# Where the routing's transpose stands in the tiles of a gated FFN

## The chip, the cores and the metric

The kernel runs on one core of one Trainium2 chip. The metric is the device time of one execution, in microseconds (us). The kernel before takes 975.53 us, the median of 3 runs (974.83 to 975.91).

## The reference, cut to what matters

The block works on one sequence of 2048 tokens with 1024 channels: half an FFN, an attention with a convolution in front, and half an FFN again. Both FFNs use the same weights and are alike. The cut below leaves the attention out.

```python
def ffn(xf):                       # xf: 2048 x 1024, after a layer norm
    routing = softmax(xf @ gate_w.T)                 # 2048 x 8
    in_scale = routing @ in_channel_scale            # 2048 x 1024
    out_scale = routing @ out_channel_scale          # 2048 x 1024
    return (xf * in_scale) @ sign(weight).T * out_scale + bias
x = x + 0.5 * ffn(layernorm(x))
x = x + attention(layernorm(x))
x = x + 0.5 * ffn(layernorm(x))
```

So each token gets a routing of 8 numbers; from it come a scale for each input channel and one for each output channel; between the two stands a product with a 1024 x 1024 matrix of signs.

## The kernel before, in words

The core's engines are TensorE (PE, with its weight loads listed as PEld), VectorE (DVE), ScalarE (ACT), GpSimd (POOL) and the DMA queues, SyncE's (SP) among them. Each engine works through its own list in order, and waits for the others by semaphores.

Each FFN is an object of the class `Ffn`. It runs over 16 tiles of 128 tokens. What is done for a tile, with the lines of the kernel before:

- `norm`: the layer norm of a row of tokens (statistics on DVE, L164 to L170; the row itself on ACT, L182).
- `transpose`: eight PE transposes of 128 x 128 (tile `tr_f`, L216), copied out by ACT (L217).
- `gate`: the gate's products, sixteen on PE in four groups of 32 columns of the array (tile `lgp_f`, L224), copied out by ACT (L232).
- `route`: one small product (L237), then the softmax on DVE and ACT (L239 to L249). The result is `rhl_f`, the routing with its rounding rest, repeated eight times.
- `turn`: one PE transpose of the routing (tile `rt_f`, L256) and one DVE copy that brings it to SBUF and rounds it (tile `rT_f`, L258). This is "the routing's turn".
- `scale`: eight small products that read `rT_f` and use 32 rows of the array each (tile `is_f`, L268), and in `out_scale` two more for the output's scale (`po_f`, L291). DVE multiplies the transposed row by the input scale (L279), ACT rounds it to the high part of `y_f` (L281), POOL makes the low part (L282). ACT writes the output scale `os_f` (L293).
- `main`: the sign products. For each half of the output channels there are 16 products of 128 x 128 by 512 columns (8 chunks, high and low part) that add up in one PSUM bank (`pm_f`, L307). Then the sums are used: DVE multiplies the bank by the output scale (L319) and adds it to the row (L320).

`run` is the loop over tiles. In step t it calls: the gate of tile t + 2, the scale of tile t + 1, `main` of tile t for half 0, the route of t + 2, the transposes of t + 3, the norm of t + 4, and then `main` of tile t for half 1. Into this second half the turn of tile t + 2 is put by the argument `beside`: a step that `main` calls ahead of a given chunk, here chunk 6 of 8, so after 12 of the 16 products. At t = 14 and 15 there is no turn left. The first FFN's first tiles are written by hand in `begin`, and its `run` starts at t = 2; the second FFN's starts at t = 0, so they make 12 and 14 of these turns.

In `begin` the order is the written one. Everywhere else the framework's scheduler sets the order of each engine's list: it goes by the written order, by its own estimate of when an operand is there, and by the buffers, and it may take later work ahead of an instruction that it expects to wait. Instructions given to `pin` keep their place. The first FFN's DVE list also has the attention's own preparations (its layer norm, L164 to L170 on `x`, and the convolution's transforms, L460 to L462); the second FFN's has none of these.

PSUM is handed out in four pools of two banks: `mm` for the sign products, `acc` for `po_f`, `tr` for the transposes and `is_f`, `sm` for `lgp_f`, the route's product and `rt_f`.

Of the kernel before, what the change touches and what calls it, by code (L numbers as in the profile page):

```python
# [24 lines left out]
def kernel(  # L25
# [28 lines left out]
    DC = D // P  # L54
# [18 lines left out]
    def bank(kind, shape, name):  # L73
        return banks[kind].tile(shape, F32, name=name, tag=kind)
# [25 lines left out]
    def pin(ins):  # L100

        tc.keep_in_program_order(ins)
# [81 lines left out]
    class Ffn:  # L184
# [108 lines left out]
                nc.scalar.mul(osc[:, ts(h, NB)], po, 0.5)  # L293
            self.oscs[t] = osc

        def main(self, t, *halves, beside={}, apart=DC):


            y, xrow = self.ys[t], self.row(t)
            pms = {h: bank("mm", [P, NB], f"pm_{self.name}_{t}_{h}") for h in halves}  # L300
            for c, h in [(c, h) for c in range(apart) for h in halves] + [
                (c, h) for h in halves for c in range(apart, DC)
            ]:
                if h == halves[0] and c in beside:
                    beside[c]()
                for n in range(2):
                    ins = nc.tensor.matmul(  # L307
                        pms[h],
                        lhsT=y[:, n, c, :],
                        rhs=self.sw[:, c, ts(h, NB)],  # L310
                        start=(c == 0 and n == 0),
                        stop=(c == DC - 1 and n == 1),
                    )
                    if self.behind:
                        pin(ins)
                        self.behind = False
                if c == DC - 1:
                    o, xt = self.oscs[t][:, ts(h, NB)], xrow[:, ts(h, NB)]
                    nc.vector.tensor_tensor(pms[h], pms[h], o, ALU.mult)  # L319
                    nc.vector.tensor_tensor(xt, xt, pms[h], ALU.add)  # L320
                    self.leave(t, h)
            if NH2 - 1 in pms:
                del self.ys[t], self.oscs[t]
# [19 lines left out]
        def run(self, first):  # L343

            self.behind = first > self.first
            for t in range(first, self.end):
                if t + 2 not in self.lgps:
                    self.on(self.gate, t + 2)  # L350
                if t + 1 < self.end:
                    self.scale(t + 1, out=True)
                self.main(t, 0)
                self.on(self.route, t + 2)
                self.on(self.transpose, t + 3)
                self.on(self.between, t - 2)
                self.on(self.norm, t + 4, t < self.kept)
                self.on(self.add_bias, t + 4)
                self.main(t, 1, beside={DC - 2: lambda: self.on(self.turn, t + 2)})
                self.on(self.after, t - 1)  # L360
                self.beside(t)

# [719 lines left out]
```

## Time and profile before

| what | value |
|---|---|
| median of 3 runs | 975.53 us |
| the profiled execution, its own time | 974.22 us |
| its span (first to last instruction) | 972.0 us |
| PE busy | 952.3 us, 98% of the span |
| DVE busy | 638.0 us, 66% |
| ACT busy | 409.6 us, 42% |
| POOL busy | 250.4 us, 26% |
| granted TensorE clock | 1.00 over the span |
| first FFN, tiles 2 to 15 | about 47 to 195 us |
| second FFN, `run` | about 813 us to the end |

A line of the timeline gives start and length in us, the engine, the line of the kernel, the operation, output <- inputs, shapes, and the count of instructions merged; in brackets the engine's idle time before it and what ended that. The chain of work that ended last is followed back from the end: a piece gives start and length in us, then engine, tile and line. PE's instructions are pipelined, so their recorded lengths overlap: what one costs is read from start to start.

### The profile page before, as it was taken

The numbers are of one execution on the slowest core, as the hardware profiler recorded it, in microseconds if no ns is written. First come the engines' busy times: TensorE is split into PE (matmuls) and PEld (weight loads), VectorE is DVE, ScalarE is ACT, GpSimd is POOL, SyncE is SP. The second block draws the span as 40 slices with busy tenths as digits, with TensorE's granted clock in tenths as the row PEclk, the third lists the DMA queues.
The fourth block names the chain that finished last, engine by engine and source line by source line (L and its number), as shares of the span: only waits on it lengthen the run. The fifth ranks groups of instructions, "written<-read, shape, count | busy, mean of one in ns | idle before, by whom it ended". The sixth has DMA issues, their size and how long they took to land.

```text
span 972.0 us, 13861 instructions
## 1 busy us (share of the span) xinstructions
PE 952.3 (98%) x5064; PEld 623.5 (64%) x5064; DVE 638.0 (66%) x1228; ACT 409.6 (42%) x1122; POOL 250.4 (26%) x319
## 2 busy tenths in 40 slices
PE   6999999999999999999999999999999999999997
PEld 4688778876666666645555455545554556878776
DVE  5788887799986566537656455646555655666654
ACT  5586665421111111126545344536451653444441
POOL 2555443410011101004213121212122312444341
PEclk9999999999999999999999999999999999999999
DMA  9776554698487665235020430044004216646331
GB/s 337 173 199 192 154 174 145 240 246 329 153 260 204 176 172 139 77 134 203 27 104 1 169 109 5 1 157 146 1 0 154 56 31 219 171 135 174 104 109 65
DMA packets 37522, 137.21 MB, mean 141 GB/s; under 512 B 4872, under 2 KB 5896, under 8 KB 35536
## 3 DMA queue, kind: packets, MB, share of 16 engines
q1 hardware_dynamic: 28336, 98.69, 27.9%
q0 software_dynamic: 8384, 29.63, 16.1%
q10 hardware_dynamic: 736, 8.02, 2.2%
q8 instruction: 40, 0.66, 0.3%
q14 instruction: 26, 0.21, 0.1%
HBM read 81.70 MB, written 37.85 MB: 123 GB/s over the span
## 4 chain that ended last, share of the span: by engine, by line
PE 60%; issue 27%; POOL 5%; DVE 3%; DMA 2%; ACT 2%; POOLq 0%; DVEq 0%; ACTq 0%
PE pm_f L307 22%; PE cv L540 22%; POOL xr L857 3%; PE tr_f L216 3%; PE pp L991 2%; PE lgp_f L224 2%; DMA x<-in_x_dram 2%; POOL p L913 2%; PE acc L972 2%; PE is_f L268 1%; PE tr L427 1%; PE pq L880 1%; PE ao L955 1%; PE pt L942 1%; DVE st_f L164 1%
## 5 line engine op out<-in xcount | busy, mean ns | idle before, releaser
L307 PE MATMUL pm_f<-sw,y_f 128*128 128x512 f32 x1024 | 261.5, 406 | 0.6 <-ACT y_f L281 0.4
L307 PEld LDWEIGHTS pm_f<-sw,y_f 128*128 128x128 f32 x1024 | 187.1, 190 | 43.9 <-ACT y_f L281 0.8
L540 PE MATMUL cv<-v,u 128*128 128x342 f32 x576 | 166.0, 450 | 0.0
L540 PEld LDWEIGHTS cv<-v,u 128*128 128x128 f32 x576 | 109.0, 189 | 56.9 <-issue 0.3
L913 POOL TENSOR_SCALAR_AFFINE_SELECT p<-p 128x512 f32<-128x512 f32 x64 | 39.8, 646 | 280.9 <-ACT p L911 280.9
L926 ACT ACTIVATE p<-p,anm 128x128 f32<-128x128 f32 x256 | 99.0, 388 | 16.7 <-DVE anm L923 16.7
L282 POOL TENSOR_TENSOR y_f<-xnT_f,y_f 128x512 fp32r<-128x512 f32 x63 | 79.8, 1282 | 64.8 <-ACT y_f L281 64.8
L319 DVE TENSOR_TENSOR pm_f<-pm_f,os_f 128x512 f32<-128x512 f32 x64 | 44.6, 697 | 70.9 <-PE pm_f L307 70.7
L557 ACT ACTIVATE m<-cv 128x342 f32<-128x342 f32 x42 | 19.2, 457 | 158.7 <-PE cv L540 148.5
L911 ACT COPY p<-sc 128x512 f32<-128x512 f32 x64 | 34.3, 588 | 111.5 <-PE sc L901 111.4
L923 DVE TENSOR_REDUCE anm<-p 128x4 f32<-128x512 f32 x64 | 40.9, 681 | 47.6 <-POOL p L913 47.6
L972 PE MATMUL acc<-oT,wo_sb 128*128 128x512 f32 x128 | 67.2, 616 | 0.4 <-DVE oT L964 0.4
L880 PE MATMUL pq<-qkv,wq_sb 128*128 128x512 f32 x128 | 61.0, 596 | 0.0
L880 PE MATMUL pq<-qkv,wk_sb 128*128 128x512 f32 x128 | 60.1, 592 | 0.0
L540 PE MATMUL cv<-v,g 128*128 128x342 f32 (+2 forms) x224 | 57.1, 415 | 0.9 <-DVE v L462 0.9
L991 PE MATMUL pp<-pw_sb,o2T 128*128 128x512 f32 x128 | 57.4, 599 | 0.4
L864 PE MATMUL pv<-wv_sb,qkv 128*128 128x512 f32 x128 | 56.1, 592 | 0.0
L217 ACT COPY xnT_f<-tr_f 128x512 f32<-128x512 f32 x62 | 35.9, 587 | 47.7 <-PE tr_f L216 47.7
L540 PEld LDWEIGHTS cv<-v,g 128*128 128x128 f32 x224 | 39.7, 190 | 17.6 <-DVE v L462 1.3
L528 DVE SCALAR_TENSOR_TENSOR u<-g,u 128x1024 f32<-128x1024 f32 x18 | 22.0, 1220 | 41.5 <-issue 23.5
L926 ACT ACTIVATION_READ_ACCUMULATOR p<-p,anm 128x1 f32 x256 | 47.8, 187 | 0.0
L934 DVE TENSOR_TENSOR p<-p,asum 128x512 f32<-128x512 f32 x64 | 45.6, 712 | 2.2
(138 smaller groups left out, 1462.7 us busy)
## 6 DMA issues: line engine op xcount, KB each, us to landing
g<-in_conv_w_dram SPq DMA_DIRECT2D x28, 512.0 KB, 4.9
u<-in_conv_w_dram POOLq DMA_DIRECT2D x24, 512.0 KB, 6.1
x<-in_x_dram SPq DMA_DIRECT2D x16, 512.0 KB, 4.6
raw<-in_weight_t_dram SPq DMA_DIRECT2D x16, 512.0 KB, 6.0
x<-hbias POOLq DMA_DIRECT2D x16, 512.0 KB, 5.5
x<-x SPq DMA_DIRECT2D x16, 512.0 KB, 4.3
xr<-x SPq DMA_DIRECT2D x16, 512.0 KB, 6.9
x<-xr SPq DMA_DIRECT2D x16, 512.0 KB, 3.2
```

The lines of the kernel that those rows point to most:

```text
L282: lows[h].tensor_tensor(yl, y, yh.bitcast(F32), ALU.subtract)
L307: ins = nc.tensor.matmul(pms[h], lhsT=y[:, n, c, :], rhs=self.sw[:, c, ts(h, NB)], start=(c == 0 and n == 0), stop=(c == DC - 1 and n == 1),)
L319: nc.vector.tensor_tensor(pms[h], pms[h], o, ALU.mult)
L540: nc.tensor.matmul(accs[w, k][:, lo:hi], lhsT=uk[:, c, :], rhs=V[k][:, c, lo:hi], start=(c == 0), stop=(c == DC - 1),)
L864: nc.tensor.matmul(pv, lhsT=qkvs[g][2][:, c, ts(b, P)], rhs=wv_sb[:, c, ts(half, NB)], start=(c == 0), stop=(c == WC - 1),)
L880: nc.tensor.matmul(pq, lhsT=w_sb[:, c, ts(hp, P)], rhs=qkvs[g][n][:, c, :], start=(c == 0), stop=(c == WC - 1),)
L913: nc.gpsimd.affine_select(out=p, in_=p, pattern=[[0, BPG], [-1, P]], compare_op=ALU.is_ge, fill=NEG_INF, base=0, channel_multiplier=1,)
L923: nc.vector.tensor_reduce(nmax, p, AX.X, ALU.max, negate=True)
L926: nc.scalar.activation(p[:, b, :], p[:, b, :], AF.Exp, bias=nmax[:, b : b + 1], accum_out=asum[:, b : b + 1],)
L934: nc.vector.tensor_tensor(p, p, asum.unsqueeze(2).broadcast_to([P, BPG, P]), ALU.mult)
L972: nc.tensor.matmul(accs[g][m], lhsT=wo_sb[:, hp, ts(m, P)], rhs=oT, start=(hp == 0), stop=(hp == NHP - 1),)
L991: nc.tensor.matmul(pp, lhsT=o2T[:, m, ts(b, P)], rhs=pw_sb[:, m, ts(h, NB)], start=(m == 0), stop=(m == WC - 1),)
```

## The change

`main` gets an argument `behind`, a step that is called after the last product of the last half and ahead of the multiplication and the addition that use its sums. `run` gives the turn of tile t + 2 to `behind`, and no longer to `beside` ahead of chunk 6. `begin` is as it was.

```diff
-        def main(self, t, *halves, beside={}, apart=DC):
+        def main(self, t, *halves, beside={}, apart=DC, behind=lambda: None):
...
                 if c == DC - 1:
+                    if h == halves[-1]:
+                        behind()
                     o, xt = self.oscs[t][:, ts(h, NB)], xrow[:, ts(h, NB)]
                     nc.vector.tensor_tensor(pms[h], pms[h], o, ALU.mult)
...
-                self.main(t, 1, beside={DC - 2: lambda: self.on(self.turn, t + 2)})
+                self.main(t, 1, behind=lambda: self.on(self.turn, t + 2))
```

How the built lists differ, for the step that turns tile 6 of the second FFN (both are built programs; "x" counts products):

```
PE before                       PE after
pm_f_4_1 x12                    pm_f_4_1 x16
rt_f_6                          rt_f_6
pm_f_4_1 x4                     lgp_f_7 (gate)
lgp_f_7 (gate)                  pm_f_5_0 x2
is_f_6, po_f_6                  is_f_6, po_f_6
pm_f_5_0 x16                    pm_f_5_0 x14

DVE before                      DVE after
rT_f_6 (L258)                   pm_f_4_1 * os (L319)
pm_f_4_1 * os (L319)            rT_f_6 (L258)
x + pm_f_4_1 (L320)             x + pm_f_4_1 (L320)
xnT_f_6 * is_f_6 (L279) x2      xnT_f_6 * is_f_6 (L279) x2
```

So besides the moved transpose, the scheduler takes two sign products of the next tile ahead of the scale's products, and puts the copy `rT_f` behind the multiplication. This is so in 13 steps of the second FFN (tiles 2 to 14) and in 11 of the first (tiles 4 to 14; three products at tile 4). At tile 15 no gate is left. In the first FFN its scale products stood behind three products of the next tile before, and do after; in the second they stood right behind the tile's last product before, and stand behind five products of the next tile after.

In the first FFN, DVE's list has three patterns. At tiles 6 and 9 the copy stays ahead of the multiplication, but behind a statistic (L164) and a transform (L462) that stood after it before. At tile 15 the copy stays where it was, ahead of the multiplication. At the others it goes behind the multiplication; there the input's scaling (L279) also goes behind the small statistics (L168, L170). On ACT the attention's layer norm of two late tiles comes ahead of the output scale; on POOL some small operations trade places. SP's list is the same.

## The prediction

> **What bounds the kernel now.** I read the page's shares first, then who waited for whom on PE, over the whole span.
>
> ```profile
> PE 952.3 (98%) x5064; PEld 623.5 (64%) x5064; DVE 638.0 (66%) x1228; ACT 409.6 (42%) x1122; POOL 250.4 (26%) x319
> ```
>
> ```profile
> PE rt_f L256 <- DVE rhl_f L249: 2.6, 3, 1.7
> ...
> PE is_f L268 <- DVE rT_f L258: 0.3, 1, 0.3
> ```
>
> PE is busy for 98% and waits for almost nothing. So what PE issues, and in which order, is the time: a stall of PE, or a slower order, is paid in full, and nothing else is. Of the waits that the change touches, `rt_f` has 2.6 us; 1.7 of that lies in the hand-written beginning, which stays, and 0.9 in two tiles of the first FFN (0.61 at 100.5 us, 0.30 at 133.5). Between 813 us and the end PE waits for nothing at all.
>
> Next, the timeline of the second FFN where the turn and the gate stand. PE and DVE lines only:
>
> ```profile
> 881.00 0.27 PE L256 MATMUL rt_f<-ident,rhl_f 128*128 128x128 f32 x1
> ...
> 881.03 1.17 PE L307 MATMUL pm_f<-sw,y_f 128*128 128x512 f32 x4
> ...
> 881.31 0.29 DVE L258 CAST rT_f<-rt_f 128x128 fp32r<-128x128 f32 x1
> ...
> 882.13 0.38 PEld L224 LDWEIGHTS lgp_f<-xnT_f,gate_sb 128*32 128x32 f32 x16 [0.36 <-issue]
> 882.13 0.64 PE L224 MATMUL lgp_f<-xnT_f,gate_sb 128*32 128x128 f32 x16
> 882.24 0.70 DVE L319 TENSOR_TENSOR pm_f<-pm_f,os_f 128x512 f32<-128x512 f32 x1 [0.63 <-PE pm_f L307]
> ...
> 882.71 0.33 PE L268 MATMUL is_f<-rT_f,tables 32*128 32x128 f32 x2
> ...
> 882.97 0.69 DVE L320 TENSOR_TENSOR xf<-xf,pm_f 128x512 f32<-128x512 f32 x1
> ...
> 883.29 4.00 PE L307 MATMUL pm_f<-sw,y_f 128*128 128x512 f32 x16
> ```
>
> To see: the copy `rT_f` is over at 881.60, 1.1 us before the scale's products read it. And where the kind of PE work changes (full array for `pm_f`, 32 columns for the gate, 32 rows for the scale), the weight load does not run ahead: the gate's first load stands idle 0.36 us and starts with its product.
>
> Last, the chain where an order like the coming one is already there. First the beginning (gate, then sign products), then the first FFN's tile 15 (sign products, scale, sign products):
>
> ```profile
> 30.04 0.57 PE lgp_f L224 x16
> 30.61 1.16 PE pm_f L307 x4
> ```
>
> ```profile
> 175.97 1.62 PE pm_f L307 x7
> 177.59 0.26 PE is_f L268 x2
> ...
> 178.19 3.22 PE pm_f L307 x13
> ```
>
> Four undisturbed products take 0.92 us (0.231 from start to start); after the gate they take 1.16. Thirteen would take 3.00; after the scale they take 3.22. A return to the full array costs some 0.2 us, whichever kind it returns from.
>
> **The change, part by part.** Starts are from single records, us.
>
> *The transpose itself.* Before, it splits the products: product to transpose 0.240, transpose to product 0.028, then 0.314 to the next; 0.582 for two steps of 0.231, so 0.12. After, it stands between the last product and the gate. Product to transpose is again 0.24. Transpose to gate is in no undisturbed row; the nearest is transpose to a row-tiled product at 795.4 us, 0.203. The 0.44 take the place of the 0.320 from product to gate: 0.12 again. I take 0 for the move. Bounds: 0.11 (the plain step of a transpose) to 0.351 (transpose to gate at 9.0 us, where the gate also waits for a copy), so -0.09 to +0.15 a tile.
>
> *The two products that come ahead of the scale.* From the 12th product to the next tile's fourth, before: 0.582 + 2 x 0.231 + 0.320 + gate 0.371 + gate to scale 0.203 + scale 0.389 + scale to product 0.201 + first to second product 0.341 + 2 x 0.231 = 3.33. After: 4 x 0.231 + 0.237 + 0.203 + 0.371 + gate to product 0.202 (30.34 us) + 0.341 + product to scale 0.327 (177.19 and 950.89 us) + 0.389 + 0.201 + 0.341 = 3.54. So +0.205 a tile, all from one more return to the full array. 24 tiles have it (11 and 13): **+4.9 us**. At tile 15 of the second FFN one split goes (the transpose out of the products, 0.12 as above) and one comes at the same price: 0.
>
> Here a rule weighs against the change of kind costing anything. "TensorE: Matmul & The Clock Gate", Part 2, says of step one that PE pulls weight loads ahead of running products where the row groups don't conflict or the spare weight buffer is the target. By that the loads would hide and the sum of this part would be 0. "TensorEngine Tiling (Array Packing)", Tiling Modes, says that changing the tiling mode drains TensorE, without a price. The 0.36 us of idle load above and the 1.16 for 0.92 decide for the second: +4.9, not 0.
>
> *The copy behind the multiplication, second FFN.* The last product starts at 881.81, the multiplication at 882.24, and the next DVE operation 0.73 later. In the changed order that is the copy: 0.43 + 0.73 + 0.29 = 1.45 after the last product's start, and a waiting PE resumes some 0.05 after a copy (rows at 90.65 and 123.89): 1.50. PE reaches the scale at 0.237 + 0.203 + 0.371 + 0.202 + 0.341 + 0.327 = 1.68. So the two products and the gate hide it, with 0.18 us to spare: 0. Were the cover gone, everything behind the scale on PE would wait. The addition comes 0.29 later; it holds up the row's store on SP, and the refill of the row, which is used tiles later. The input's scaling on DVE starts some 0.6 later, and so do ACT's rounding and POOL's low part; that low part ends at 887.82, and PE wants it at 893.28. Covered.
>
> *The same in the first FFN, where DVE lags.* The view of DVE there:
>
> ```profile
> 122.97 0.67 DVE L462 TENSOR_TENSOR v<-v,xw 128x512 f32<-128x512 f32 x1
> 123.56 0.28 DVE L258 CAST rT_f<-rt_f 128x128 fp32r<-128x128 f32 x1
> 123.77 0.68 DVE L319 TENSOR_TENSOR pm_f<-pm_f,os_f 128x512 f32<-128x512 f32 x1
> ```
>
> The transform runs into the turn. Tile 10, before: PE stalls 0.1 for `rT_f`. After: transform to 123.57, multiplication to 124.25, copy to 124.54, PE free again at 124.59; PE arrives at 122.90 - 0.12 (the transpose no longer ahead) + 1.68 = 124.46, a stall of 0.14. The same working gives 0.1 at tile 7, 0.12 and 0.16 at tiles 6 and 9 (copy behind L164 and L462), 0.3 at tile 4 (copy over at 59.46, arrival 59.20); tiles 5, 8 and 11 to 15 have no lag or an arrival after the copy. Sum **+0.8**, for the 0.2 that go (tiles 7 and 10): +0.6. Bounds: 0, if DVE's list closes up, to 0.3 in all 11 tiles, 3.3.
>
> *The stall that goes.* `rt_f` waited for `rhl_f`, whose DVE list waited for a row's load. The transpose now comes some 0.9 us later than the 12th product, more than either stall: **-0.9**. The load's issue follows the addition on SP, and at tile 7 multiplication and copy only swap, so it is not later. Bounds -0.9 to 0.
>
> No DMA is moved and SP's list is unchanged. Nothing past the FFNs moves: PE is busy without gaps in the convolution and the attention, so the shift passes through.
>
> **The sum.** +4.9 + 0.6 - 0.9 = +4.6 on the profiled execution: 974.22 becomes 978.8, its span 972.0 becomes 976.6. The median lies 1.3 above that execution, and I add the same: **980.1 us**, 0.47% slower.
>
> **Rivals.**
>
> *The copy is late in every tile.* The cover is only 0.18 us in the second FFN and none in the lagging tiles. If multiplication and copy take 0.2 longer than read, PE waits at the scale. For: the copy is now behind 0.7 us of DVE work that before came after it. Against: both durations are from rows. At 0.1 to 0.3 in 24 tiles, 2.4 to 7.2 more: 982.5 to 987.
>
> *The extra change of kind is free* (the pull-ahead rule). Then +0.6 - 0.9 = -0.3: 975.2, no change. It decides when a split costs under 0.09 us a tile (24 x 0.09 is 2.2, less 0.3 gives the 0.2% that a measurement tells from no change, 1.95 us). Against it: 1.16 for four products.
>
> *The change does nothing.* The transpose's move alone costs 0 by the sum above; if the two products had not come ahead, the time would be 974.6 to 975.5. The built order says they do.
>
> *A smaller cost:* DVE's lag closes up and the stalls go, or the transpose in front of the gate drains with it: 24 x (0.205 - 0.09) - 0.9 = +1.9, so 977 to 978.5.
>
> **Chances.** The forecast 0.72 (its own range 978.5 to 982.3), the late copy 0.12, the free change 0.05, nothing done 0.03, the smaller cost 0.08. Range: leaving out the two that end at no change and the upper end of the late copy gives 977.8 to 983.2. Slower by over 0.2% takes the forecast, the late copy and most of the smaller cost: 0.90; within 0.2% 0.08; faster 0.02, for which no mechanism of that size is in the profile.
>
> **What would show it.** In the second FFN, products from tile to tile start 10.19 us apart, for 9.99 before; the chain shows gate, two products, scale, fourteen products, with 0.2 us over in both groups of products; PE has no wait for `rT_f`. In the first FFN the two waits for `rhl_f` are gone, and short waits for `rT_f` stand at tiles 4, 6, 7, 9 and 10. The prediction is wrong if PE waits for `rT_f` in the second FFN, if gate to product and back takes less than 0.1 over, or if the transpose in front of the gate has another price than 0.12.

## The result, and the profile after

The changed kernel takes 978.47 us (median of 6 runs, 978.28 to 979.26), the kernel before 974.75 us in the runs beside it (974.14 to 975.91). The ratio is 1.0042, with a 95% interval of 1.0032 to 1.0052: slower by 0.4%. The profiled execution took 978.28 us, its span is 976.0 us, for 974.22 and 972.0 before: +4.06 and +4.0, where the prediction had +4.6.

Lines from L318 on are two higher now: the multiplication is L321, the addition L322. First the page's shares, then who waited for whom on PE over the whole span (us in all, times, the longest).

```profile
span 976.0 us, 13847 instructions
...
PE 954.8 (98%) x5064; PEld 622.7 (64%) x5064; DVE 634.8 (65%) x1228; ACT 409.9 (42%) x1122; POOL 253.6 (26%) x319
```

```profile
PE rt_f L256 <- DVE rhl_f L249: 2.3, 2, 1.6
PE is_f L268 <- DVE rT_f L258: 2.2, 3, 0.9
```

PE has the same 5064 instructions and is still busy for 98%. Its busy time grew by 2.5 us, which isn't the 4.0 of the span: the records overlap, so only starts tell what an order costs. The granted clock is 1.00 from 52 to 195 us and from 813 to 972 us in both profiled executions, so the difference isn't the clock's. Both waits for `rhl_f` that remain lie in the beginning; between 47 and 202 us there is none, where before there were two of 0.9 us together. Of the three for `rT_f`, two lie in the beginning; the third, 0.9 us, is new, at tile 15 of the first FFN. From 813 us on PE has no wait for either.

The timeline of the second FFN at the turn of tile 8 (tiles count from 0), cut to PE, its weight load for the gate, and DVE:

```profile
884.79 0.27 PE L256 MATMUL rt_f<-ident,rhl_f 128*128 128x128 f32 x1
884.99 0.38 PEld L224 LDWEIGHTS lgp_f<-xnT_f,gate_sb 128*32 128x32 f32 x16 [0.29 <-issue]
885.00 0.70 DVE L321 TENSOR_TENSOR pm_f<-pm_f,os_f 128x512 f32<-128x512 f32 x1 [0.83 <-PE pm_f L307]
885.00 0.65 PE L224 MATMUL lgp_f<-xnT_f,gate_sb 128*32 128x128 f32 x16
...
885.57 0.73 PE L307 MATMUL pm_f<-sw,y_f 128*128 128x512 f32 x2
885.60 0.28 DVE L258 CAST rT_f<-rt_f 128x128 fp32r<-128x128 f32 x1
885.80 0.68 DVE L322 TENSOR_TENSOR xf<-xf,pm_f 128x512 f32<-128x512 f32 x1
886.23 0.33 PE L268 MATMUL is_f<-rT_f,tables 32*128 32x128 f32 x2
```

The copy `rT_f` is over at 885.88, behind the multiplication, and PE reaches the scale at 886.23. So the late copy costs nothing here, and it is the gate and the two products that hide it. The chain of the same place shows what is paid instead:

```profile
881.23 3.73 PE pm_f L307 x16
884.96 0.11 PE rt_f L256
885.07 0.57 PE lgp_f L224 x16
885.64 0.66 PE pm_f L307 x2
886.30 0.26 PE is_f L268 x2
886.55 0.11 PE po_f L291
886.66 0.23 PE is_f L268 x5
886.89 3.46 PE pm_f L307 x14
```

Sixteen products without a break take 3.73, or 0.233 each. Two between gate and scale take 0.66 for 0.47, and fourteen behind the scale 3.46 for 3.26. So each return to the full array costs 0.2, and a turn now has two of them. Tile to tile the second FFN steps by 10.160 us, for 9.987 before: +0.173.

By stages, from landmarks on PE in the two profiled executions (us):

| stage | before | after | change |
|---|---|---|---|
| start to the route's product of tile 4 of the first FFN | 51.46 | 51.08 | -0.39 |
| from there to the convolution's first product | 143.37 | 145.25 | +1.88 |
| convolution and attention | 618.56 | 618.90 | +0.35 |
| second FFN, first to last sign product | 153.22 | 155.46 | +2.24 |
| behind it | 5.40 | 5.29 | -0.11 |

The whole cost lies in the two FFNs. The first row and the third are not the change's: they differ from run to run in every trace below. The third does so with PE's wait for the attention's `pT` ahead of `ao`: 0.7 us in all before, 1.0 after, 1.9 in a second trace of the same changed kernel, up to 2.7 below. That moves totals by 1 to 2 us, so the experiments are read by steps and windows of their traces first, and by their medians second.

### The profile page after: what moved, and what is told of

Same layout as the page of the kernel before. It is cut to its first block, busy times and chain, and to the rows that moved or that the text cites. A ratio compares the mean times of both kernels' runs of the same rounds, so it can differ in the third digit from the quotient of the medians.

```text
span 976.0 us, 13847 instructions
## 1 busy us (share of the span) xinstructions
PE 954.8 (98%) x5064; PEld 622.7 (64%) x5064; DVE 634.8 (65%) x1228; ACT 409.9 (42%) x1122; POOL 253.6 (26%) x319
## 4 chain that ended last, share of the span: by engine, by line
PE 60%; issue 27%; POOL 5%; DVE 4%; ACT 2%; DMA 1%; POOLq 0%; DVEq 0%; ACTq 0%
PE pm_f L307 23%; PE cv L542 22%; POOL xr L859 3%; PE tr_f L216 3%; PE pp L993 2%; POOL p L915 2%; PE lgp_f L224 2%; PE is_f L268 2%; PE acc L974 2%; PE tr L429 1%; PE pq L882 1%; PE ao L957 1%; DVE st_f L164 1%; PE pt L944 1%; PE po_f L291 0%
## 5 line engine op out<-in xcount | busy, mean ns | idle before, releaser
L321 DVE TENSOR_TENSOR pm_f<-pm_f,os_f 128x512 f32<-128x512 f32 x64 | 44.6, 698 | 74.6 <-PE pm_f L307 74.4
L279 DVE TENSOR_TENSOR xnT_f<-xnT_f,is_f 128x512 f32<-128x512 f32 x64 | 41.1, 681 | 9.5 <-PE is_f L268 9.5
```

The costliest lines, as they stand in the source:

```text
L279: nc.vector.tensor_tensor(y, y, sc, ALU.mult)
```

## The experiments

The theory: the cost is the further return to the full array, because two products stand between gate and scale. The rivals: the transpose's new place costs, or the copy's place behind the multiplication does. In the second FFN each can be had without the others, and DVE has nothing else in the way there. Times are set against the kernel before on the same chip (975.67 to 976.18 us).

**The move alone.** The transpose goes behind the last product, but `pin` keeps the next tile's products behind the scale and the copy ahead of the multiplication. Against the kernel before (`self.running` is true inside `run`):

```diff
-        def main(self, t, *halves, beside={}, apart=DC):
+        def main(self, t, *halves, beside={}, apart=DC, behind=lambda: None):
...
+                    if h == halves[-1]:
+                        behind()
-                    nc.vector.tensor_tensor(pms[h], pms[h], o, ALU.mult)
+                    ins = nc.vector.tensor_tensor(pms[h], pms[h], o, ALU.mult)
+                    if self.running and h == 1:
+                        pin(ins)
...
+                self.behind = True      # pins the tile's first product
                 self.main(t, 0)
...
-                self.main(t, 1, beside={DC - 2: lambda: self.on(self.turn, t + 2)})
+                self.main(t, 1, behind=lambda: self.on(self.turn, t + 2))
```

The route's product is pinned as well.

> The turn stands behind the last sign product as in the changed kernel, but the next tile's first sign product is kept behind the scale's products, and the copy of the turn is kept ahead of the multiplication of the sums; nothing is left out. Theory (each further return from small array tiles to the full array costs some 0.17 to 0.2 us): no further return, so the second FFN's tiles are 9.99 us apart as before, and the time is that of before less the two waits for the routing in the first FFN (0.9): 974.0 to 974.9 where before is 974.75. Rival (the late transpose itself costs the time): about 978.5, and the second FFN's tiles 10.16 us apart.

Measured: 977.61 us, ratio 1.0015 (1.0009 to 1.0022). The second FFN steps by 9.985 us, as before: the move itself costs nothing there. The total is above the theory's expectation, and the waits on PE between 47 and 202 us tell why:

```profile
PE is_f L270 <- DVE rT_f L260: 2.9, 4, 0.8
```

In the first FFN, DVE's other work makes the copy late even when it stands ahead of the multiplication, and without the two products PE has only the gate to do meanwhile. Three steps there take 11.69 to 11.73 us for 10.73, and the window is 144.75 for 143.37. At tile 15 of the second FFN, where there is no gate, PE waits 0.38 as well. So the two products cost time and also buy cover.

**The split alone.** All is as before, but the scale stands behind the next tile's first two products:

```diff
+        def scale_all(self, t):
+            self.scale(t, out=True)
...
-                if t + 1 < self.end:
-                    self.scale(t + 1, out=True)
-                self.main(t, 0)
+                self.main(t, 0, beside={1: lambda: self.on(self.scale_all, t + 1)})
```

> The kernel before, its turn where it was, but the scale of the next tile is written behind the first two sign products of a tile; nothing is left out. Theory: one more return to the full array at 27 tiles (12 and 15), each 0.17: 4.6 more, up to 0.9 more for a late stall in the first FFN's tile 15, and up to 0.5 less for a shorter wait for the routing: 978.9 to 980.4; second FFN's tiles 10.16 apart. Rival (the transpose's and the copy's new place costs the time): 974.8, tiles 9.99 apart.

The chain's piece between gate and scale:

```profile
889.77 0.66 PE pm_f L310 x2
```

Measured: 982.12 us, ratio 1.0060 (1.0048 to 1.0072). The two products take 0.66, as in the changed kernel, and the second FFN steps by 10.183: +0.196 a tile with the transpose and the copy in their old places, more than the whole +0.173 of the change. The total went past the expectation. Part of that is the attention's `ao`, which waited 2.7 us in this trace; another is the first FFN (146.59 for 143.37), where the waits of `rt_f` for `rhl_f` not only stay but grow (1.6 us in 4 turns, for 0.9 in 2) beside the dearer turns.

**Gate and scale together, behind the two products.** The same shift of the scale, but the gate goes along with it, so that there is again one return:

```diff
+        def gate_and_scale(self, t):
+            if t + 2 not in self.lgps:
+                self.on(self.gate, t + 2)
+            if t + 1 < self.end:
+                self.scale(t + 1, out=True)
...
-                if t + 2 not in self.lgps:
-                    self.on(self.gate, t + 2)
-                if t + 1 < self.end:
-                    self.scale(t + 1, out=True)
-                self.main(t, 0)
+                self.main(t, 0, beside={1: lambda: self.gate_and_scale(t)})
```

The gate's first product is pinned.

> The kernel before, its turn where it was, but gate and scale together are written behind the first two sign products of a tile; nothing is left out. Theory (the count of returns to the full array decides): one return a tile as before, so 974.3 to 975.8 (the upper end with the late stall at tile 15 of the first FFN), second FFN's tiles 9.99 apart. Rival (what costs is that a half's sixteen products are broken into two and fourteen): as with the split alone, 979 to 980, tiles 10.16 apart.

Measured: 977.53 us, ratio 1.0013 (1.0005 to 1.0021); the second FFN steps by 9.987. So neither the two products nor the scale behind them cost, only the split between gate and scale. The median is 1.6 over before, above the 974.3 to 975.8 expected. In the trace the first FFN is longer by as much (144.93 for 143.37), and `rt_f` waits there for `rhl_f` 1.9 us in 4 turns, 1.0 more than before.

**The changed kernel with ACT's old order.** In the changed kernel the attention's layer norm of rows 11 and 12 (tile `x2n`) had come ahead of the FFN's work on ACT. Here `pin` holds it:

```diff
+            ins = nc.scalar.activation(dst, src, AF.Identity, bias=shift, scale=rstd)
+            if name in ("x2_11", "x2_12"):
+                pin(ins)
```

> The changed kernel with one thing more: on ScalarE the attention's layer norm of the rows 11 and 12 is kept in its written place, so that it no longer stands ahead of the output scale of tiles 13 and 14; nothing is left out. Theory (that norm delays the routing of tile 15, whose copy is then 0.9 us late for the scale): 0.9 less than the changed kernel, 977.6, and no wait of over 0.2 us at tile 15 of the first FFN. Rival (VectorE's transforms alone make the copy late there): 978.5, wait of 0.9 still there.

To see what is at stake, first the chain of the changed kernel at the first FFN's tile 15, and PE's line there:

```profile
170.73 1.25 ACT x2n L182
171.97 0.97 ACT os_f L293 x2
172.94 1.02 ACT y_f L281 x2
173.96 0.50 ACT xw L433
174.46 0.26 ACT ro_f L242 x2
...
175.50 0.63 DVE rhl_f L248
...
176.88 0.69 DVE v L463
177.57 0.60 DVE v L462
178.17 0.60 DVE v L464
178.77 0.21 DVE rT_f L258
```

```profile
179.03 0.33 PE L268 MATMUL is_f<-rT_f,tables 32*128 32x128 f32 x2 [0.92 <-DVE rT_f L258]
```

The norm takes 1.25 us on ACT ahead of `os_f`, and before it ACT sits idle until POOL has the norm's shift:

```profile
170.73 1.25 ACT L182 ACTIVATE x2n<-x,sh_x,rs_x 128x1024 f32<-128x1024 f32 x1 [2.69 <-POOL sh_x L181]
```

The run with the pins is the one to compare with: its PE is at the same place to 0.07 us until 172.2 us. There `os_f` starts at 168.99, here at 171.88. So the softmax's `ro_f` starts at 174.34 for 173.41, `rhl_f` is over at 176.96 for 175.51, and the convolution's transforms that stand between it and the copy on DVE are late with it. PE waits 0.92.

Measured with the pins: 978.56 us, ratio 1.0025 (1.0016 to 1.0033), for 1.0042 and, on another chip below, 1.0041 of the changed kernel. The step of the second FFN is the same 10.160. In the first FFN PE has no listed wait for `rT_f` or `rhl_f` left, and the window is 143.93 instead of 145.25: -1.3. Of this 0.98 is the start of the scale at tile 15, and 0.25 the attention's transposes on PE just ahead of that tile's products, for which the trace names no wait.

**The changed kernel again,** unaltered, as a base on the chip of the next runs:

> The changed kernel again, so that the others of this set have it on the same chip: 3.7 to 4.3 over before; second FFN's tiles 10.16 us apart; wait of 0.9 for the copy of the turn at tile 15 of the first FFN.

Measured: 980.2 us, ratio 1.0041 (1.0027 to 1.0054); step 10.160, first FFN 145.19, the wait at tile 15 again 0.9. The first result repeats in each part.

**The changed kernel with one return.** Transpose and copy stay as changed; gate and scale go together behind the two products (`gate_and_scale` as above), and `x2n` is pinned:

```diff
-                if t + 2 not in self.lgps:
-                    self.on(self.gate, t + 2)
-                if t + 1 < self.end:
-                    self.scale(t + 1, out=True)
-                self.main(t, 0)
+                self.main(t, 0, beside={1: lambda: self.gate_and_scale(t)})
```

> The changed kernel, its turn behind the last sign product and its copy behind the multiplication, but with the gate written together with the scale behind the first two products of the next tile, so that there is one return to the full array a tile, and with the attention's norm of rows 11 and 12 kept in place on ScalarE; nothing is left out. Theory (the return is what costs): second FFN's tiles 9.99 apart, no waits for the routing and none over 0.3 for the copy: 0.9 less than before to 0.2 more than before. Rival (late transpose and copy cost): tiles 10.16 apart, 3 to 4 over before.

The chain at the same turn of the second FFN:

```profile
879.84 3.73 PE pm_f L321 x16
883.57 0.11 PE rt_f L264
883.68 0.47 PE pm_f L321 x2
884.15 0.57 PE lgp_f L230 x16
884.72 0.26 PE is_f L276 x2
884.98 0.11 PE po_f L305
885.08 0.23 PE is_f L276 x5
885.31 3.46 PE pm_f L321 x14
```

Measured: 975.66 us, ratio 0.9997 (0.9989 to 1.0005): the time of before, with the moved transpose and the late copy still in it. Against the changed kernel's chain one piece differs: the two products take 0.47, not 0.66. The step is 9.985. In the first FFN, PE waits for `rT_f` 1.1 us in 3 turns, about what it had waited for `rhl_f` before; one of the waits is 0.6, over the 0.3 expected.

**The copy without cover.** The changed kernel, with the next tile's first product pinned behind the scale; the copy stays behind the multiplication:

```diff
-            self.behind = first > self.first
+            self.behind = self.running = True
...
+                self.behind = True
                 self.main(t, 0)
```

(The route's product is pinned too.)

> The changed kernel with the next tile's first sign product kept behind the scale, and the copy of the turn left behind the multiplication: no further return, and no cover for the copy; nothing is left out. By the rows PE reaches the scale 1.01 us after the last product's start and the copy lets it go at 1.50: 0.49 a tile at 14 tiles of the second FFN, its tiles 10.48 apart, and 0.5 to 1.0 at 11 or 12 of the first: 11 to 18 over before. If instead the copy's place costs nothing: as before.

Chain and waits:

```profile
880.90 0.70 DVE pm_f L323
881.60 0.20 DVE rT_f L260
881.80 0.04 issue
881.84 0.33 PE is_f L270 x2
```

```profile
PE is_f L270 <- DVE rT_f L260: 10.9, 27, 1.6
```

Measured: 986.92 us, ratio 1.0110 (1.0096 to 1.0124). PE waits in every turn (10.9 us in 27 waits, one of them in the beginning), the second FFN steps by 10.35, +0.37: gate to scale takes 0.570 from start to start, for 0.203. This is the wait that the prediction's first rival feared, made here by taking the cover away, and at 10.7 us over before it is dearer than the changed kernel. It is a little under the 11 to 18 expected: the step was to grow by 0.49, from the same reading of DVE that made the prediction's slack too small (below).

**Two splits.** All as before, but the scale's eight products in two parts, behind two and behind four products of the next tile:

```diff
-                if t + 1 < self.end:
-                    self.scale(t + 1, out=True)
-                self.main(t, 0)
+                self.main(t, 0, beside={1: lambda: self.on(self.scale_half, t + 1), 2: lambda: self.on(self.scale_rest, t + 1)})
```

(`scale_half` issues four of them, `scale_rest` the other four and the output scale's two.)

> The kernel before, its turn where it was, with the scale's products in two parts, behind two and behind four sign products: two more returns to the full array a tile instead of one; nothing is left out. Theory: twice the 0.196 that the single split showed, so the second FFN's tiles 10.37 to 10.40 apart, and 4.5 to 6 over the single split, 10 to 12 over before. If the drain overlaps with the next change of kind: under 10.25 apart.

```profile
885.74 0.66 PE pm_f L316 x2
886.40 0.37 PE is_f L267 x4
886.76 0.66 PE pm_f L316 x2
887.43 0.26 PE is_f L267 x2
887.68 0.11 PE po_f L300
...
887.80 3.06 PE pm_f L316 x12
```

Measured: 991.9 us, ratio 1.0161 (1.0147 to 1.0175); the second FFN steps by 10.587, +0.60. The expectation was twice the first split, 10.37 to 10.40, and it failed: the second split costs 0.40 alone. By the chain: 0.19 on its two products as before, and beyond that the broken scale takes 0.75 in its two parts for 0.60 in one, and the last twelve products 3.06 for 3.46 less two of 0.233, which is 0.07.

Read from start to start, the single split takes PE from gate to product in 0.203, to the second product in 0.336 and to the scale in 0.327; without it, PE goes from gate to scale in 0.203 and through two products at 0.233 each. That is +0.197, the whole of the step's +0.196. So the first split added one change of kind, from gate to product: that from the gate to the scale was there already, and that from products to the scale took its place. The second split cuts through products of one kind and adds two changes, out of the scale and back into it. So a split is not one fixed price.

**One return, and the copy ahead of the multiplication.** As the one-return kernel, with the multiplication pinned behind the copy:

```diff
-                    nc.vector.tensor_tensor(pms[h], pms[h], o, ALU.mult)
+                    ins = nc.vector.tensor_tensor(pms[h], pms[h], o, ALU.mult)
+                    if self.running and h == 1:
+                        pin(ins)
```

> The grouped kernel of the last set (gate and scale together behind the first two products of the next tile, turn behind the last product) with the copy of the turn kept ahead of the multiplication of the sums; nothing is left out. Theory (the 1.1 us that PE still waits for the copy at three tiles of the first FFN comes from the multiplication ahead of it): those waits go, the first FFN from its fifth tile on takes 142.0 to 142.5 us where the kernel before takes 143.4, and the time is 0.9 to 1.5 under before. Rival (VectorE's other work makes the copy late whatever stands ahead): as the grouped kernel, no difference to before.

Measured: 976.03 us, ratio 1.0005 (0.9997 to 1.0014); step 9.985. The waits for `rT_f` in the first FFN don't go, they move from tiles 4, 7 and 10 to 4, 6 and 9 (1.3 us in 3): there a statistic or a transform stands ahead of the copy. So the multiplication isn't what makes those copies late. No version was measurably faster than the kernel before.

Steps of the second FFN, all in one table (us from tile to tile):

| PE's order between two tiles | copy ahead of the multiplication | copy behind it |
|---|---|---|
| gate, scale, 16 products | 9.985 (9.987 before, transpose in its old place) | 10.35 |
| gate, 2 products, scale, 14 products | 10.183 (transpose in its old place) | 10.160, the change |
| 2 products, gate, scale, 14 products | 9.985 (9.987 with the transpose in its old place) | 9.985 |

The first row says that a late copy costs 0.37 without cover; the second, that a split costs 0.17 to 0.20 wherever the copy is; the third, that the cover can be had without the split.

## Why the prediction was right, point by point

The forecast was 980.1 us, range 977.8 to 983.2; it came to 978.47. That is just under the 978.5 to 982.3 that the prediction gave its own account, and inside the 977 to 978.5 of its rival *a smaller cost*. Half of this rival came true (DVE's lag closed up, and the stalls went), half did not (a step of +0.173 and not +0.115). By the terms of the sum on the span (us):

| term | predicted | measured |
|---|---|---|
| further return, 13 turns of the second FFN | +2.67 | +2.24 |
| further return, 11 turns of the first | +2.26 | +1.9 (11 x 0.173) |
| stalls for the copy at tiles 4, 6, 7, 9, 10 | +0.8 | +0.22 |
| stalls at tiles 7 and 10 that go | -0.2 | -0.2 (gate to scale 0.288 and 0.300 before, for 0.203) |
| waits for `rhl_f` that go | -0.9 | -1.3 |
| ACT's order, tile 15 | 0 | +1.3 |
| the other stages | 0 | -0.15 |
| sum | +4.6 | +4.0 |

*The transpose at no cost:* right. The step with the move alone is 9.985 for 9.987. The row that the prediction missed, transpose to gate undisturbed, does stand in the trace before, at 790.91 us: 0.202, for the 0.203 that it borrowed from another row; the changed kernel has 0.202.

*One more return a tile:* the mechanism is shown, by the split alone (+0.196) and by its undoing in the changed kernel (10.160 to 9.985). Its size was 0.03 too high. Gate to product took 0.202 as read; the first to the second product took 0.338 for 0.341, and product to scale 0.319 for 0.327. Such differences of some thousandths, of rows from other places, add up over ten terms. The rule of the Trainium skill's "TensorEngine Tiling (Array Packing)", Tiling Modes, that a change of the tiling mode drains TensorE, was the right one to follow: a change of kind has a price, 0.17 to 0.20 us a split here. The traces show the price and not the drain itself. The other rule that the prediction weighed, weight loads pulled ahead, would have made it free; the engine of the weight loads sat idle for 0.29 ahead of the gate's first.

*The copy hidden in the second FFN, with 0.18 to spare:* hidden, yes, but the slack is 0.29 (0.34 from the copy's end to the scale, less the 0.05 that a waiting PE needs). The prediction took 0.73 from the multiplication to the next DVE operation. That was read from the addition, which needs the multiplication's result. The copy doesn't, and starts 0.60 behind it, before its end.

*The stalls of the first FFN:* the step that failed. Of five tiles named, only tile 4 has one (0.22 for 0.3). At tiles 6, 7, 9 and 10 the copy is over 0.19 to 0.41 ahead of the scale. DVE's lag closed up, the bound of 0 that the prediction gave. At tile 10 the sum had DVE begin the multiplication 0.79 behind the last product's start, and it begins 0.61 behind; the copy then follows after 0.60 and not 0.68, the misreading above. The sum took DVE's starts from the trace of before, while PE's turn became 0.17 longer; that this accounts for all of the lag isn't shown. At tile 15, put down as nothing, PE waits 0.92. The built lists had shown that a norm on ACT comes ahead of the output scale of a late tile, and no cost was put on it; the pins show that it is worth 1.3 in the window. The norm's own 1.25 on ACT was not all: ACT also stood idle for its input, with other work ready behind it. A reordering on an engine that is busy for 42% reached PE, through ACT's list, the softmax and DVE's list.

*The waits that go:* they went, and took more than their 0.9 along. The two long tiles of before, taken from the first product of half 1 to the next tile's, were 11.60 and 11.25 us where those around them take 10.75 to 10.91; in the changed kernel all of these are 10.94 to 10.97. The waits were listed as 0.61 and 0.30. The list counts idle time from the recorded end of the product before, and by then the next one would already have started. From start to start the transpose took 0.999 and 0.684 behind its product, for about 0.235 in undisturbed turns, so it came 0.76 and 0.45 late; and the product behind it followed after 0.086 and 0.085, for 0.028. That is 0.82 and 0.50, or 1.3 in all.

The errors in the first FFN (stalls -0.6, the waits -0.4, tile 15 +1.3, the return's size -0.35) nearly cancel: its window grew by 1.88 for 1.96 predicted. That sum was right by luck, with the wrong parts in it.

*From the span to the median:* 1.3 was added, as the median before lay above its profiled execution. With six runs of each, it lies 0.5 above it before and 0.2 after. This is two thirds of the 1.6 us between forecast and result.

## What to carry to other kernels

Read the built order of the engine that bounds, and count how often in a loop's turn it goes from small tiles of the array back to full ones: a change that moves no work at all between engines cost 0.4% because a scheduler filled a gap with two products between two groups of small ones. When such a filler is also what hides a late operand, don't take it away (here +1.1%), but move both small groups behind it. And put a price on every reordering that the built lists show, on the idle engines too, by following what is queued behind it and what it has to wait for itself.

## What was not expected of the hardware

- An operation on DVE that doesn't need the result of the one ahead of it starts before that one's end: 0.60 us behind the start of a 0.70 us multiplication, where one that needs it starts 0.73 behind.
- A second split of PE's order costs twice the first (0.40 for 0.20): it adds two changes of kind, out of a group of small products and back into it, where the first put one in another's place and added one.
- A wait of PE that is listed as 0.61 us made the next product 0.82 late, one of 0.30 us 0.50.
- An operation that comes ahead in ACT's list can block it for longer than it runs: with a norm of 1.25 us ahead of it `os_f` started 2.9 us later, because ACT stood idle for the norm's input first.
